# Four small re-arrangements around interleaved selective scans in an eight-image conv, attention and state-space kernel

## The chip, the cores and the metric

The kernel runs on one core of a Trainium2 chip, on a batch of eight images. The metric is the device time of one execution in microseconds (us), lower is better. A core has five instruction queues that the text names by their engine: PE (TensorE, matrix products, with its weight loads PEld), DVE (VectorE), ACT (ScalarE), POOL (GpSimd) and SP (SyncE, which here only issues DMAs). DMAs of convolution and projection weights are issued from ACT's queue, nearly all others from SP's.

## The reference

Each image has 256 channels and 32 x 32 = 1024 positions. Four residual layers follow one another; the first three see a group norm of their input.

```python
x = x + attention(gn(x))            # layer 0: 8 heads of 64, l2-normed q and k
x = x + conv3x3(gn(x), w1)          # layer 1
x = x + conv3x3(gn(x), w2)          # layer 2
x = x + mixer(gn(x))                # layer 3
# mixer(x): xs = x as 1024 tokens of 256 channels
xn = layernorm(xs)
xm = [mamba(xn[:, 64*i:64*i+64]) + skip * xn[...] for i in range(4)]   # 4 branches
Q  = gates from xm;  r = projections and depthwise convs of xm * sigmoid(Q), and of xs
xm2 = project(cat(xs, r)) + xs
x_out = cat(conv1d(xm2), mha(xm2)) @ fc_w.T + fc_b
out = project(layernorm(depthwise3x3(ln_hw(gelu(layernorm(x_out))))))
# mamba: u, z = xs @ inw;  u = silu(conv1d(u));  dt = softplus(...u...);  B, C = ...u...
#   h[t] = exp(dt[t]*A) * h[t-1] + dt[t]*u[t]*B[t];  y[t] = sum_s C[t]*h[t] + u*D   (16 states)
```

All arithmetic is in 32-bit floats.

## The kernel before

**Layers and stages.** For one image the front is `front_attention` and `front_convs` (layers 0 to 2). Then `scan_layers` norms the image and runs the four mamba branches. Then come `back_layers` (gates, projections, the mixer's attention), `back_out` (the `fcw` projection) and `back_end` (gelu, norms, the 3x3 depthwise convolution and the last projection). Front and back layers are "dense": PE carries most of them. A loop over images `b` puts the scans of image `b` beside the front of image `b + 1` and the back of image `b - 1`. For the last image (`b` = 7, counted from 0) there is no further front, so its scans stand beside the back of image 6 alone; the back of image 7 is written after all that.

**Handing out the scans.** `interleave(dense, scans, pace)` walks the dense stream, whose steps yield an estimated cost, and takes one step of the scan stream each time that the cost spent has grown by `pace`. `PACE` has one value per image: 1.8, then 2.78 six times, then 1.6. Within a queue, an instruction of a scan step is kept behind the dense instruction written ahead of it (`Paced`, `held`). Beyond that a scheduler decides the order on each engine when the program is built; on the chip every engine works through its list in order.

**Scans.** A scan works on 32 channels x 4 states in 128 partitions and 512 positions. A branch has 16 units: two halves `h` of the positions, four groups `q` of states, two pairs `gp` of channel groups. A unit takes: `load` and `load_dt` (DMAs of `du`, `bc` and `dt` from memory), `drive` (POOL, line 974: `hs = du * B`), `decays` (ACT: two times `da = exp(dt * A)` into PSUM), `scan` (DVE: two scans of 512), `weigh` (POOL, lines 1005 and 1006: keep the last state in `carry`, then `hs = hs * C`), and `add_up` (PE: `y += hs`). Tiles of `du` and `dt` are loaded once per half (at `q == 0`), one for each `gp`, and serve four units each; so units 0, 1 and 8, 9 of a branch load them, four DMAs for each tile. Each stage runs some units ahead:

```python
for ahead, stage in (
    (3, load), (1, load_dt), (0, decays), (0, None),
    (0, scan), (-1, weigh), (2, drive),
):
```

**A branch's front.** `branch_front` makes what the scans load, in six steps: project, convolve to `u`, `low` (B and C, stored as `bc`, line 865), `a` and an exponential, step sizes `dt` (stored as `dt_m`, line 818), and `dt * u` (stored as `du_m`, line 818). `fronts` gives the steps of the next branch due times in units of the running scans. `branch_back` multiplies by the gate `z` and projects once a branch has ended. Stores and loads of the scans, the small DMAs of the attentions (`sums`, `both`, `inv`, `rs`) and `mix` all stand in SP's one queue.

**The mix tensor.** `back_layers` ends with four 128 x 1024 tiles: two of the local convolution, two of the attention (`o3`). They are stored to memory as `mix` (line 1312), and `back_out` loads them again (line 1379) as input of the `fcw` projection. For images in the middle there is a whole front attention between the two.

**Buffers.** `wsp` (weight chunks), `hp` (`half_work`: the tiles `rs0` and `both`, which DMAs read), `dtp` (tiles `du` and `dt`, two each), `hsp` (six), `tp` (twelve 128 x 1026 tiles for nearly all dense work).

All of PE's, DVE's and ACT's instructions are issued through one wrapper and carry line 105 in the profile; there the tile names tell them apart.

Of the kernel before, what the change touches and what calls it, by code (L numbers as in the profile page):

```python
# [11 lines left out]
F32 = mybir.dt.float32  # L12
# [7 lines left out]
P = 128  # L20
C = 256
N = 1024
HALF = 512
# [10 lines left out]
def preact_stack(ctx: ExitStack, tc: tile.TileContext, I, out, cols):  # L34
# [7 lines left out]
    wp = ctx.enter_context(tc.tile_pool(name="wp", bufs=1))  # L42
    sp = ctx.enter_context(tc.tile_pool(name="sp", bufs=2))

    wsp = ctx.enter_context(tc.tile_pool(name="wsp", bufs=6))
    xp = ctx.enter_context(tc.tile_pool(name="xp", bufs=1))
    vp = ctx.enter_context(tc.tile_pool(name="vp", bufs=1))
    tp = ctx.enter_context(tc.tile_pool(name="tp", bufs=12))
    hp = ctx.enter_context(tc.tile_pool(name="hp", bufs=2))
    ps_big = ctx.enter_context(tc.tile_pool(name="ps_big", bufs=2, space=PSUM))  # L50
    ps_acc = ctx.enter_context(tc.tile_pool(name="ps_acc", bufs=1, space=PSUM))

# [11 lines left out]
    def work(name):  # L64
        return tp.tile([P, TP], F32, tag="t", name=name)
# [10 lines left out]
    def mwork(name):  # L76
        return mp.tile([P, N], F32, tag="m", name=name)
# [4 lines left out]
    def da_tile():  # L82
        return ps_da.tile([P, HALF], F32, tag="da", name="da")
# [730 lines left out]
    def store(br, name, src):  # L814

        br[name] = dp.tile([32, 2, 4, HALF], F32, tag=name, name=name + "_m")
        for h in range(2):
            nc.sync.dma_start(
                out=br[name][:, h].rearrange("d g n -> g d n"), in_=src[:, HALVES[h]]
            )  # L820

    def branch_front(i, xn, br):


        j, rows = i // 2, slice((i % 2) * 64, (i % 2) * 64 + 64)
        for h in range(2):
            ps = da_tile()
            tensor.matmul(
                ps,
                minw[rows, j, 0:P],  # L830
                inner(xn[j])[rows, HALVES[h]],
                start=True,
                stop=True,
            )
            scalar.copy(raw[:, 3 + h * HALF : 3 + (h + 1) * HALF], ps)
        yield
        u = mp.tile([P, N], F32, tag="u", name="u", bufs=2)
        uu = u[:, 0:N]
        scalar.activation(
            uu,  # L840
            raw[:, 3 : 3 + N],
            AF.Identity,
            bias=col("convb", i),
            scale=col("convw", 4 * i + 3),
        )
        for k in range(3):
            vector.scalar_tensor_tensor(
                uu, raw[:, k : k + N], col("convw", 4 * i + k), uu, ALU.mult, ALU.add
            )
        th = raw[:, 3 : 3 + N]  # L850
        scalar.activation(th, uu, AF.Tanh, scale=0.5)
        vector.scalar_tensor_tensor(uu, th, 1.0, uu, ALU.add, ALU.mult)
        br["u"] = u
        yield

        low = mwork("low")
        for h in range(2):
            ps = da_tile()
            tensor.matmul(
                ps[0 : 2 * DS], mxpw[:, i], u[:, HALVES[h]], start=True, stop=True  # L860
            )
            scalar.copy(low[0 : 2 * DS, HALVES[h]], ps[0 : 2 * DS])
        br["bc"] = dp.tile([DS, 2, 2, HALF], F32, tag="bc", name="bc")
        for k in range(2):
            nc.sync.dma_start(
                out=br["bc"][:, :, k],
                in_=low[k * DS : (k + 1) * DS].rearrange("s (h n) -> s h n", h=2),
            )
        yield

        a, dt = mwork("a"), mwork("dt")
        aa, ee, dd = a[:, 0:N], raw[:, 3 : 3 + N], dt[:, 0:N]
        for h in range(2):
            ps = da_tile()
            tensor.matmul(
                ps, mdtw[:, i], u[:, HALVES[h]], start=True, stop=True
            )
            vector.tensor_scalar_add(a[:, HALVES[h]], ps, col("dtb", i))  # L880
        scalar.activation(ee, aa, AF.Abs)
        scalar.activation(ee, ee, AF.Exp, scale=-1.0)
        yield
        vector.tensor_scalar_add(dd, ee, 1.0)
        vector.scalar_tensor_tensor(ee, dd, -1.0, ee, ALU.add, ALU.subtract)
        scalar.activation(dd, dd, AF.Ln)
        vector.tensor_sub(dd, dd, ee)
        vector.scalar_tensor_tensor(dd, aa, 0.0, dd, ALU.max, ALU.add)
        store(br, "dt", dd)
        yield  # L890
        vector.tensor_mul(aa, dd, uu)
        store(br, "du", aa)
        yield

    def branch_back(i, xn, br):
# [27 lines left out]
    def scan_steps(branches):  # L923
# [14 lines left out]
        def load_groups(u, name):  # L938
            br, g = branches[u["i"]], u["gp"] * 2
            if u["q"] == 0:  # L940
                t = dtp.tile([P, 2, HALF], F32, tag=name, name=name)
                src = br[name][:, u["h"], g : g + 2].rearrange("d g n -> d (g n)")
                for s in range(4):
                    nc.sync.dma_start(
                        out=t[s * 32 : s * 32 + 32].rearrange("d g n -> d (g n)"),
                        in_=src,
                    )
                br[name, u["gp"]] = t
            u[name] = br[name, u["gp"]]
# [80 lines left out]
        for n in range(-3, len(units) + 2):  # L1030
            done = None
            for ahead, stage in (
                (3, load), (1, load_dt), (0, decays), (0, None),
                (0, scan), (-1, weigh), (2, drive),
            ):
                if stage is None:
                    yield
                elif 0 <= n + ahead < len(units):
                    stage(units[n + ahead])
            if n % 2 and 0 <= n - 3 < len(units) - 1:  # L1040
                done = add_up(units[n - 3 : n - 1])
            yield done

    def scan_layers(img):


        xt = img.pop("x")
        img["stats"] = group_stats(img.pop("mv"), da_tile)
        xn = [xm_tile("xn0"), xm_tile("xn1")]
        for t in xn:  # L1050
            zero_ends(t)
        group_norm(tiles(xt), img["stats"], [inner(t) for t in xn])
        img["xd"] = xdp.tile([P, 2, N], F32, tag="xd", name="xd")
        nc.sync.dma_start(out=img["xd"], in_=xt)
        sq = [mwork("ln_sq"), mwork("ln_sq")]
        yield
        yield from layer_norm(
            [inner(t) for t in xn], sq, BY_HALF, da_tile, affine("norm_w", "norm_b")
        )
        yield  # L1060
        branches = [{} for _ in range(NB)]
        for _ in branch_front(0, xn, branches[0]):
            yield

        def fronts():
            for i in range(1, NB):
                for n, _ in enumerate(branch_front(i, xn, branches[i])):
                    yield 16 * i - 12 + 9 * n // 4

        front, ending, due, n = fronts(), iter(()), 0, 0  # L1070
        steps = scan_steps(branches)
        while True:
            next(ending, None)
            while due is not None and n >= due:
                due = next(front, None)
            if next(steps, END) is END:
                break
            yield
            done = next(steps)
            if done is not None:  # L1080
                ending = branch_back(done, xn, branches[done])
            n += 1
            yield
        yield from ending
        img["xm"] = xn
# [123 lines left out]
    def back_layers(img, exact=False):  # L1209
# [82 lines left out]
        yield from project("fpw", fd, evac_x2)  # L1292


        img["mix"] = xdp.tile([4, P, N], F32, tag="mix", name="mix")
        local = []

        def add_local():
# [9 lines left out]
                next(img["begin"])  # L1308
        while len(local) < 2:
            add_local()  # L1310
        for t, part in enumerate(local + img.pop("o3")):
            nc.sync.dma_start(out=img["mix"][t], in_=part[:, 0:N])

    def merge_weights():

# [58 lines left out]

    def back_out(img):

        srcs = [work("mix")[:, 0:N] for _ in range(4)]
        for t in range(4):
            nc.sync.dma_start(out=srcs[t], in_=img["mix"][t])
        yield 0  # L1380
        xo = img["xo"] = [work("xo")[:, 0:N] for _ in range(2)]

        def evac_fc(m, ps):
            scalar.activation(xo[m], ps, AF.Identity, bias=fc_b[:, m : m + 1])

        yield from project_both("fcw", srcs, evac_fc)
# [124 lines left out]
    PLACES = [1, 4, 4, 4, 4, 5, 6, 8, 9, 10, 11, 12, 13, 14, 15, 16]  # L1511
    PLACES += [18, 20, 22, 24, 26, 27, 28, 29]
    EARLY = 3
    PACE = [1.8] + [2.78] * (batch - 2) + [1.6]
    imgs = [{} for _ in range(batch)]
    drain(
        amid(front_attention(image_of(0), imgs[0]), merge_weights(), (8,)),
        front_convs(imgs[0]),
# [51 lines left out]
    again = nc.values_load(flag[0:1, 0:1], min_val=0, max_val=1)  # L1570
    with tc.If(again > 0):
        with tc.For_i(0, batch, 1) as i:
            img = {}
            src = x_in[bass.ds(i, 1)].rearrange("o (t p) n -> p (o t) n", p=P)
            dst = out[bass.ds(i, 1)].rearrange("o c n -> (o c) n")
            drain(front_attention(src, img, True), front_convs(img), scan_layers(img))
            drain(back_layers(img, True), back_out(img), back_end(img, dst))
# [109 lines left out]
```

## Time and profile before

| what | value |
|---|---|
| median of 3 runs | 6550.79 us (6543.21 to 6555.45) |
| the profiled execution's own time | 6534.17 us |
| its span in the trace | 6532.5 us |
| PE, DVE, ACT, POOL busy | 5503.0, 4003.1, 2701.2, 2737.3 us |
| clock granted to PE, mean | 0.91 of full speed |
| moved by DMA | 496 MB, 76 GB/s |

Busy time is summed per engine and averages over stages with different limits. The span begins with 375 us of the front of image 0 alone; seven stages with scans beside dense work follow, and one stage with dense work alone. A wait is put down to the engine whose event ended it. A record `x4` is four instructions of one kind merged; a 32-bit matmul shows as two.

### The profile page before, as it was taken

The page shows a single profiled execution, that of the slowest core. Times are in us where ns is not written, and L with a number is a line of the kernel's source. Part 1 is how long each engine was busy: PE and PEld are TensorE (multiplying, and loading weights), DVE is VectorE, ACT ScalarE, POOL GpSimd, SP SyncE. Part 2 cuts the span into 40 slices and gives each one's busy share as a digit, 9 for nine tenths or more (in the row PEclk, how much of TensorE's full clock was granted, in tenths as well). Part 3 has the DMA queues.
Part 4 walks back from the last instruction along what each step waited for, and adds up shares of the span by engine and source line. Part 5 has one row for each costly group of instructions (what it writes and reads, how often), then busy time and mean ns, then how long its engine had stood idle before and what let it go on. Part 6 is the DMA issues. An engine that isn't in the chain of part 4 may idle for free.

```text
span 6532.5 us, 52259 instructions
## 1 busy us (share of the span) xinstructions
PE 5503.0 (84%) x17318; PEld 1846.7 (28%) x17318; DVE 4003.1 (61%) x4613; ACT 2701.2 (41%) x3241; POOL 2737.3 (42%) x1302
## 2 busy tenths in 40 slices
PE   8886688899888988989889898899889898876496
PEld 2331133223332233222332233322332223311222
DVE  5247845577556775567756776567855777555622
ACT  3223424644255532644236442555326442344242
POOL 0006653634435353543517345263435435276500
PEclk9997889999899989999899998999899998988697
DMA  1022232323233132321223222231323212233301
GB/s 44 26 62 76 78 89 76 88 74 88 69 91 98 39 93 77 101 85 57 81 82 99 75 75 80 83 103 44 91 77 101 87 57 82 77 82 88 97 26 43
DMA packets 224761, 495.99 MB, mean 76 GB/s; under 512 B 61016, under 2 KB 102616, under 8 KB 223456
## 3 DMA queue, kind: packets, MB, share of 16 engines
q1 hardware_dynamic: 168032, 419.12, 22.2%
q10 hardware_dynamic: 56448, 73.43, 3.9%
q8 instruction: 139, 2.28, 0.1%
q14 instruction: 142, 1.16, 0.1%
HBM read 411.09 MB, written 72.88 MB: 74 GB/s over the span
## 4 chain that ended last, share of the span: by engine, by line
PE 53%; DVE 24%; issue 6%; DMA 6%; ACT 6%; POOL 4%; SPq 1%; ACTq 0%; DVEq 0%; POOLq 0%
PE big L105 33%; PE acc L105 11%; DVE hs L105 6%; PE da L105 5%; DVE p L105 4%; DVE dw L105 3%; POOL hs L1006 3%; PE y L105 3%; DVE u L105 2%; DVE t L105 1%; DMA du_m<-a 1%; POOL hs L974 1%; ACT p L105 1%; ACT da L105 1%; DMA dt<-dt_m 1%
## 5 line engine op out<-in xcount | busy, mean ns | idle before, releaser
L974 POOL TENSOR_TENSOR hs<-du,bc 128x1024 f32<-128x1024 f32 x512 | 1339.7, 2636 | 1623.2 <-DMA du<-du_m 683.0
L1006 POOL TENSOR_TENSOR hs<-hs,bc 128x1024 f32<-128x1024 f32 x512 | 1303.7, 2547 | 1027.7 <-DVE hs L105 841.2
L105 ACT ACTIVATE p<-big 128x1024 f32<-128x1024 f32 x1024 | 1038.5, 1021 | 735.0 <-PE big L105 724.2
L105 PE MATMUL acc<-p,v 128*64 128x512 f32 x4096 | 1151.8, 636 | 8.8 <-ACT both L105 6.0
L105 ACT ACTIVATE da<-dt,a_neg 128x512 f32<-128x512 f32 x1024 | 684.2, 686 | 1144.7 <-DVE hs L105 442.1
L105 PE MATMUL big<-im,w 128*128 128x512 f32 x2304 | 1104.0, 631 | 20.4 <-ACT im L105 20.4
L105 DVE TENSOR_TENSOR p<-p 128x1024 f32<-128x1024 f32 x448 | 720.0, 1607 | 295.2 <-ACT p L105 201.8
L105 DVE TENSOR_TENSOR_SCAN hs<-da,carry,hs 128x512 f32<-128x512 f32 x512 | 623.5, 1265 | 256.4 <-ACT da L105 176.0
L105 DVE TENSOR_TENSOR_SCAN hs<-da,hs 128x512 f32<-128x512 f32 x512 | 599.7, 1209 | 286.6 <-ACT da L105 267.6
L105 PE MATMUL big<-qk,qk 64*128 64x512 f32 x2048 | 647.9, 663 | 95.2 <-ACT p L105 85.5
L105 PE MATMUL y<-hs,sel 128*32 128x512 f32 x2048 | 454.0, 674 | 315.3 <-POOL hs L1006 314.8
L105 PE MATMUL big<-q,k 64*128 64x512 f32 x2048 | 616.8, 660 | 107.2 <-ACT p L105 60.6
L105 PEld LDWEIGHTS big<-im,w 128*128 128x128 f32 x2304 | 446.9, 201 | 689.5 <-issue 642.1
L1005 POOL COPY carry<-hs 128x2 f32<-128x2 f32 x256 | 104.2, 407 | 823.0 <-DVE hs L105 745.0
L105 PEld LDWEIGHTS acc<-p,v 128*64 128x64 f32 x4096 | 213.7, 137 | 820.3 <-issue 719.0
L105 PEld LDWEIGHTS big<-qk,qk 64*128 64x128 f32 x2048 | 178.2, 192 | 537.1 <-issue 280.1
L105 PEld LDWEIGHTS big<-q,k 64*128 64x128 f32 x2048 | 165.8, 190 | 535.5 <-issue 252.6
L105 DVE SCALAR_TENSOR_TENSOR dw<-xo,vec,dw 128x961 f32<-128x961 f32 (+1 forms) x128 | 247.8, 1972 | 16.4 <-ACT dw L105 15.2
L105 PEld LDWEIGHTS y<-hs,sel 128*32 128x32 f32 x2048 | 58.6, 112 | 616.7 <-POOL hs L1006 456.4
L105 PE MATMUL big<-xn,w 128*128 128x512 f32 x512 | 230.1, 601 | 0.0
L105 DVE SCALAR_TENSOR_TENSOR u<-raw,vec,u 128x1024 f32<-128x1024 f32 x96 | 136.2, 1419 | 87.1 <-ACT u L105 85.3
L105 PE MATMUL big<-w,xn 128*128 128x512 f32 x256 | 137.2, 687 | 42.6 <-ACT big L105 34.9
(214 smaller groups left out, 5085.5 us busy)
## 6 DMA issues: line engine op xcount, KB each, us to landing
bc<-bc SPq DMA_DIRECT2D x1024, 128.0 KB
du<-du_m SPq DMA_DIRECT2D x512, 128.0 KB
dt<-dt_m SPq DMA_DIRECT2D x512, 128.0 KB
w<-in_wc ACTq DMA_DIRECT2D x192, 192.0 KB
rs<-inv SPq DMA_DIRECT2D x64, 256.0 KB
dt_m<-dt SPq DMA_DIRECT2D x64, 256.0 KB
du_m<-a SPq DMA_DIRECT2D x64, 256.0 KB
mix<-mix SPq DMA_DIRECT2D x32, 512.0 KB
```

The source lines that it names most:

```text
L105: made = issue(*args, **kwargs)
L974: nc.gpsimd.tensor_mul(u["hs"], u["du"], both_groups(u["bc"][:, 0]))
L1005: nc.gpsimd.tensor_copy(carry[:, u["q"], g : g + 2], hs[:, :, HALF - 1])
L1006: nc.gpsimd.tensor_mul(hs, hs, both_groups(u["bc"][:, 1]))
```

## The change

- Weight chunks have five buffers for six, `half_work` tiles one for two. The tag `dt` gets three buffers for two; `du` keeps two.
- In `branch_front` the step that makes and stores `bc` is moved from third to last place.
- `load_dt` runs two units ahead for one.
- The due times of a branch's front, relative to its first unit, are listed as `FRONT`: -12, -10, -8, -7, -6, -2. Before they were -12, -10, -8, -6, -3, -1. A due time is that of the step after the one it is listed with.
- With `direct` set (images 6 and 7 of the eight), `back_layers` hands its four tiles to `back_out` on the chip, and `mix` is neither stored nor loaded.
- The last value of `PACE` is 1.1 for 1.6.

```diff
-    wsp = ctx.enter_context(tc.tile_pool(name="wsp", bufs=6))
+    wsp = ctx.enter_context(tc.tile_pool(name="wsp", bufs=5))
-    hp = ctx.enter_context(tc.tile_pool(name="hp", bufs=2))
+    hp = ctx.enter_context(tc.tile_pool(name="hp", bufs=1))
...
     def branch_front(i, xn, br):
...
         br["u"] = u
         yield
-        low = mwork("low")
...
-        yield
         a, dt = mwork("a"), mwork("dt")
...
         store(br, "du", aa)
         yield
+        low = mwork("low")
...
+        yield
...
-                t = dtp.tile([P, 2, HALF], F32, tag=name, name=name)
+                bufs = 3 if name == "dt" else 2
+                t = dtp.tile([P, 2, HALF], F32, tag=name, name=name, bufs=bufs)
...
-                (3, load), (1, load_dt), (0, decays), (0, None),
+                (3, load), (2, load_dt), (0, decays), (0, None),
...
-                for n, _ in enumerate(branch_front(i, xn, branches[i])):
-                    yield 16 * i - 12 + 9 * n // 4
+                for at, _ in zip(FRONT, branch_front(i, xn, branches[i])):
+                    yield 16 * i + at
...
-        img["mix"] = xdp.tile([4, P, N], F32, tag="mix", name="mix")
+        if not img.get("direct"):
+            img["mix"] = xdp.tile([4, P, N], F32, tag="mix", name="mix")
...
-        for t, part in enumerate(local + img.pop("o3")):
-            nc.sync.dma_start(out=img["mix"][t], in_=part[:, 0:N])
+        parts = [t[:, 0:N] for t in local + img.pop("o3")]
+        if img.get("direct"):
+            img["mix"] = parts
+            return
+        for t, part in enumerate(parts):
+            nc.sync.dma_start(out=img["mix"][t], in_=part)
...
     def back_out(img):
-        srcs = [work("mix")[:, 0:N] for _ in range(4)]
-        for t in range(4):
-            nc.sync.dma_start(out=srcs[t], in_=img["mix"][t])
+        srcs = img["mix"]
+        if not img.get("direct"):
+            srcs = [work("mix")[:, 0:N] for _ in range(4)]
+            for t in range(4):
+                nc.sync.dma_start(out=srcs[t], in_=img["mix"][t])
...
-    PACE = [1.8] + [2.78] * (batch - 2) + [1.6]
-    imgs = [{} for _ in range(batch)]
+    FRONT = (-12, -10, -8, -7, -6, -2)
+    PACE = [1.8] + [2.78] * (batch - 2) + [1.1]
+    imgs = [{"direct": b >= batch - 2} for b in range(batch)]
```

More of the change, by code (lines that the diff above doesn't have):

```diff
@@ L854, in branch_front @@
         yield
-        low = mwork("low")
[L857 to L868, printed above, removed]
-        yield
         a, dt = mwork("a"), mwork("dt")
@@ L892, in branch_front @@
         store(br, "du", aa)
+        yield
+        low = mwork("low")
+        for h in range(2):
+            ps = da_tile()
+            tensor.matmul(
+                ps[0 : 2 * DS], mxpw[:, i], u[:, HALVES[h]], start=True, stop=True
+            )
+            scalar.copy(low[0 : 2 * DS, HALVES[h]], ps[0 : 2 * DS])
+        br["bc"] = dp.tile([DS, 2, 2, HALF], F32, tag="bc", name="bc")
+        for k in range(2):
+            nc.sync.dma_start(
+                out=br["bc"][:, :, k],
+                in_=low[k * DS : (k + 1) * DS].rearrange("s (h n) -> s h n", h=2),
+            )
         yield
@@ L1572, in preact_stack @@
         with tc.For_i(0, batch, 1) as i:
-            img = {}
+            img = {"direct": True}
             src = x_in[bass.ds(i, 1)].rearrange("o (t p) n -> p (o t) n", p=P)
```

## The prediction, made before the changed kernel was run

> **What bounds the kernel now.** I read the page's header and slices first, then the busy table by stretches, then the waits, then the queue and engine timelines around single waits. The storing of each image's scan input (`xd<-xt`, line 1054, at 375, 1029, 1805, 2570, 3340, 4101, 4862 and 5624 us) cuts the span into stages.
>
> ```profile
> span 6532.5 us, 52259 instructions
> ...
> PE   8886688899888988989889898899889898876496
> ...
> POOL 0006653634435353543517345263435435276500
> ```
>
> PE is nearly full up to the 37th slice, then falls to 6, 4, 9, 6. The busy table says how much (columns: stretch, length, then busy us with counts for PE, PEld, DVE, ACT, POOL, then granted clock, DMA share, GB/s):
>
> ```profile
> 4101.20:4862.40 761.20, 670.46 (x2160) 225.63 (x2160) 505.64 (x573) 337.07 (x406) 343.93 (x160) 0.94 0.28 81
> ...
> 5623.70:6207.50 583.80, 376.15 (x1156) 119.17 (x1158) 334.85 (x346) 231.02 (x285) 320.19 (x159) 0.78 0.31 87
> 6207.50:6532.50 325.00, 246.58 (x812) 90.95 (x812) 82.30 (x127) 107.29 (x106) 4.53 (x2) 0.85 0.10 33
> ```
>
> A middle stage is bound by PE (670 of 761 us, so some 90 us idle). The last scanned image is not: PE has 376 of 584 us and POOL, the scans' busiest engine, 320. That stretch is a chain of scans through ACT, DVE, POOL, PE and the queue of SP, with the back layers of image 6 (counted from 0) woven in. After it the back layers of image 7 run alone, 325 us. The waits:
>
> ```profile
> PE y L105 <- POOL hs L1006: 314.8, 114, 19.7
> ...
> ACT da L105 <- DMA dt<-dt_m: 276.0, 26, 26.6
> ```
>
> ACT, which also makes the attention's `p` for PE, stands 276 us behind step sizes. Why, SP's timeline shows at one of them, with ACT's line below it:
>
> ```profile
> 5752.03 1.17 SPq L818 DMA_DIRECT2D dt_m<-dt  x2
> 5753.25 2.60 SPq L959 DMA_DIRECT2D bc<-bc  x4
> 5755.96 7.52 SPq L944 DMA_DIRECT2D dt<-dt_m  x8
> ```
> ```profile
> 5764.52 1.30 ACT L105 ACTIVATE da<-dt,a_neg 128x512 f32<-128x512 f32 x2 [16.45 <-DMA dt<-dt_m]
> ```
>
> The loads that unit 8 of a branch needs (its second half) stand in SP's queue behind the store of the next branch's step sizes, which waits for DVE. The same happens at 5882 and 6005 us.
>
> **The Trainium skill.** "DMA: Bandwidth & Descriptors", section "Anatomy of one DMA", says that a DMA's semaphore wait is spent on the issuing sequencer before dispatch; the fence above agrees, since the loads are issued only after the waiting store. "TensorE: Matmul & The Clock Gate", Part 1, says that an idle window of about 3.4 us halves the clock; the trace agrees (four `y` records take 1.05 us in a busy stretch, 1.92 after 10 us of idleness), so idle PE costs a little more than itself. "GPSIMD Engine Reference", section 4.1, calls POOL about twice as slow as DVE on two inputs; here 2.36 us against 1.22 for 128x1024. "Perfetto Trace Analysis", section "Optimization Strategy", says that regular bubbles can mean too few buffers; that fits the two `dt` tiles, both in use until the half's last two units.
>
> **The change, part by part.**
>
> *Order of a branch's front, due times, third `dt` tile, loads two units ahead.* No instruction is added. In the written order of instructions DVE now finishes a branch's step sizes before it takes the `y` of the half (line 1029), where it took that `y` in between at branches 2 and 3 of the last image; so the drain scans, `y`, step sizes, store, load, `da` is cut. The `du` store moves with it. On SP both stores, and after them the `bc` store, now stand ahead of the last `du` loads and of the `dt` loads of the second half, so a late DVE would hold POOL instead. They stand there two units before use (about 10 us of POOL work), against the some 10 us that store and load take (5752.0 to 5764.5, with the loads between). I take most of each drain off: POOL's idle time there, 14.6 and 12.1 us, plus some lag of ACT.
>
> In the middle stages PE hardly feels this. In the stage 4101 to 4862 I can tie to `dt` only the 6.05 us at 4375 (ACT late with `big`) and perhaps half of the 9.6 us at 4200; the largest wait, 10.05 us at 4689, comes from DVE busy with `dw`. Taken: 5 us for each of six stages, 30 us; bounds -2 and +15 each. In the first stage with scans (375 to 1029, 167 us of PE idleness, 80 us of ACT waiting for `dt`): 10 us, bounds -5 and +40.
>
> *Five weight tiles for six, one `half_work` for two.* A convolution uses a chunk every 5.2 us, so four loads ahead are still 21 us; the waits show PE held by no weight load. A `both` or `rs` copy comes every eight attention steps (16.5 us apart at least), and its DMAs take about 4. Cost 0; the cover is gone if SP stands longer than that, and then ACT and PE wait. Bounds -10 and +40 us in all, within the low end below.
>
> *Inputs of the last projection kept on the chip (images 6 and 7).* 16 DMAs of 512 KB go, no instruction comes. For image 7:
>
> ```profile
> 6414.10 2.79 PE L105 MATMUL acc<-p,v 128*64 128x512 f32 x12
> 6430.01 15.58 PE L105 MATMUL big<-mix,w 128*128 128x512 f32 x32 [13.11 <-issue]
> ```
>
> Three quarters of these matmuls need only `local` and the first `o`, ready at 6417. The last quarter needs the `o` that DVE finishes at 6429.5, and 3 us of PE after that: done at 6432.5 instead of 6445.6, a gain of **13 us**. For image 6 it is in the sum below.
>
> *Pace 1.6 to 1.1.* This is the large item, with both signs. At 1.6 the scans (148 steps, 237 of cost) outlast the 226 that the back layers of image 6 add up to. At 1.1 they ask for 163 and are handed out inside the attention. The order of PE's instructions in the changed program bears it out: the last `y` stand among the `fcw` matmuls, and then all of `back_end` of image 6 comes before the first matmul of image 7's back layers. So the end is a sum in series. With E the end of the last scan on DVE (6209 us before):
>
> - last scan to the last `xn` of the branch, 6209.0 to 6223.3: 14.3
> - `few_inv` to `o`, now behind it on DVE, 6422.1 to 6429.5: 7.4
> - the last `fcw` matmuls: 3
> - `back_end`, alone on PE, 6445.6 to 6523.4 as image 7 shows: 77.8
> - back layers of image 7, first `qdw` matmul to the end, 6221.8 to 6532.5: 310.7, less 13.1
>
> Together 400.1. It pays if E falls below 6132. Before, from 5716.5 us, the halves of eight units took 49, 49, 82, 46, 76, 62, 86 and 42 us; POOL needs 39 (2 x 2.36 and a copy). The halves of 76 and 82 hold a drain and about twelve attention steps; those of 62 and 86 were held by `back_out` and by `back_end`'s `dw` on DVE. In the new order the second half's `y` have no attention between, the third and fifth keep their branch front (about 15 us of DVE and ACT in a row), and the last has fourteen attention steps of 2.1 us. I take 47, 42, 55, 43, 55, 43, 47, 53: E = 6101.5, end 6501.6, a gain of **31 us**. Bounds for E: 6065 (every half near POOL's 43) and 6150 (fronts and drains as before).
>
> Sum: 31 + 30 + 10 = 71 us off the profiled 6532.5, so 6461; its own time is 6534.17. The median of the runs, 6550.79, lies 16.6 above that; against it: **6480 us**.
>
> **The rivals.**
> (a) *Only the end counts*: a PE-bound stage gives ACT's waits back elsewhere, middle 0. For it: PE's named waits are mostly not on `dt`. Gain 31: 6520.
> (b) *The middle gains in earnest*: the 20 us waits for `dt` also delay the `y` on PE (28 to 29 us a stage). At 15 us for six stages, 25 in the first and 31: 146, so 6405. Against it: those `y` mostly follow DVE's `dw`.
> (c) *Slower*: the scans do not keep the denser pace, because DVE's and ACT's order, not the number handed out, sets it. The 78 us in which `back_end` of image 6 now stands alone on PE are then not repaid. Decides from E = 6132; with the old halves to unit 48 (6081), then 47 and 40, E is 6168 and the end 36 us later: 6587. For it: POOL idled 10 us at 5806 and 12 at 5844 with no late DMA. Against it: at 1.6 it was the attention between the scans that held them.
> (d) *Not what it says*: the third tile may be idle because SP's queue, not the tile, holds the load. Then the drains stay (some 27 us), E is about 6128, nothing comes in the middle: 6546.
>
> **How the numbers follow.** Forecast 0.45, (a) 0.2, (b) 0.15, (c) 0.12, (d) 0.08. The range runs from (b), 6405, to 6555, which takes in (d) and the mild part of (c). A measurement of this kernel tells about 0.2% (13 us) from no change. Faster by more: the forecast, (a), (b) and little of (d), 0.83; within: 0.06; slower: 0.11, nearly all of (c).
>
> **What would show it.** Right: the waits of `da` on `dt` fall from 276 us to well under 150; no `mix` DMA in the last two images; the last scan ends near 6100, less what the earlier stages gained; then about 80 us with PE at a third or less; the stages stay near 755. Wrong: `du` waits on POOL inside an image where `dt` waits were; ACT waiting for `sums` or weights; a scan stretch still longer than 416 us; or back layers of the two images overlapping after all.

## The result and the profile after

| | before | after |
|---|---|---|
| median of four runs | 6547.0 us | 6601.33 us |
| range | 6533.63 to 6555.45 | 6598.77 to 6612.32 |
| span of the profiled execution | 6532.5 us | 6600.8 us |
| clock granted to PE | 0.910 | 0.906 |

The ratio is 1.0083 (95%: 1.0065 to 1.01): the change made the kernel 0.8% slower, where the prediction had 1% faster. The experiments below split this: the third tile with earlier loads, the smaller pools and the kept inputs alone make the kernel 1.5% faster; the due times and the pace take that and more.

The page's header and slices of the kernel after:

```profile
span 6600.8 us, 52312 instructions
...
PE   8886688998889979899789988899798897856686
...
POOL 0007653634345252644526344352535435277400
```

The hole near the end is still there: where PE's digits were 7, 6, 4, 9 they are 5, 6, 6, 8. Cut by the store of the scan input, the stages took these times (the last column is a kernel of the experiments):

| stage (image of the scans) | before | after | front_pace_undone |
|---|---|---|---|
| 0 | 653.6 | 660.4 | 644.3 |
| 1 | 776.5 | 762.3 | 745.8 |
| 2 to 6, mean | 763.7 | 776.3 | 760.4 |
| 7 | 908.8 | 923.3 | 881.7 |

Of the 68 us that the span grew, 63 arose in stages 2 to 6, 14.5 in the last and 7 in stage 0; stage 1 gave 14 back. The busy table of the kernel after (columns as before: stretch, length, busy us with counts for PE, PEld, DVE, ACT and POOL, clock, DMA share, GB/s) shows a middle stage and the two halves of the last one:

```profile
4119.50:4899.30 779.80, 676.35 (x2160) 228.41 (x2160) 500.04 (x573) 337.72 (x406) 341.63 (x160) 0.93 0.28 79
5677.50:6195.30 517.80, 353.68 (x1022) 93.64 (x1022) 287.05 (x273) 212.39 (x269) 318.82 (x159) 0.78 0.31 82
6195.30:6600.80 405.50, 289.22 (x944) 120.11 (x944) 120.70 (x200) 125.66 (x123) 3.75 (x2) 0.81 0.09 26
```

The middle stage has the same instructions as before (2160 matmuls, 160 on POOL). Of its 18.6 us, 12.7 are PE's idleness (103.4 for 90.7); in the other 5.9 PE does the same matmuls at a clock of 0.93 for 0.94. In the last stage the last scan began 517.8 us after the start of the stage, and ended 66.2 us sooner than before; but 405.5 us followed its beginning, and what followed its end was 80.7 us longer than before.

The waits of ACT, a part of the list (total, times, longest):

```profile
ACT da L105 <- PE big L105: 293.8, 32, 21.1
...
ACT da L105 <- DMA bc<-bc: 170.4, 11, 17.0
...
ACT da L105 <- DMA dt<-dt_m: 142.5, 23, 27.2
...
ACT low L105 <- PE da L105: 104.7, 28, 10.0
```

The sign that the prediction had asked for seems to be there: `da` waits for `dt` 142.5 us for 276.0. But the list names only one releaser for each wait, and in the kernel before it hides another:

```profile
4703.05 13.48 ACTq L159 DMA_DIRECT2D w<-in_wc  x3
4716.74 1.30 ACT L105 ACTIVATE da<-dt,a_neg 128x512 f32<-128x512 f32 x2 [20.11 <-DMA dt<-dt_m]
```

ACT goes on 0.2 us after weight loads that it issued itself (`ACTq` is the queue on which ACT issues the chunks of weights). Eight of the 26 waits put down to `dt` before, 167.0 of the 276.0 us, end in this way, all in middle stages and stage 0, with 16 to 27 us each. After, two of those put down to `dt` do (49.1 us), and all eleven put down to `bc` (170.4; before it was 47.5 of 67.9). Waits that end with ACT's own loads are thus 214.5 us before and 219.5 after, and what is left of the waits for `dt` is 109.0 before and 93.4 after. So the sign came about mostly because waits of one kind got another name. The rest of the list doesn't tell why the kernel is slower either: front_pace_undone of the experiments, which is faster than both, has 142.3 us behind `dt` and 261.3 for PE, where the kernel after has 142.5 and 293.8 and the kernel before 276.0 and 173.9. A wait that is gone from the list is no gain until the stage is shorter.

What became of the drain in the last image, SP's timeline shows (start, duration, queue, line, operation, number of DMAs), and ACT's below it:

```profile
6020.56 0.36 SPq L945 DMA_DIRECT2D dt<-dt_m  x1
6042.85 1.23 SPq L818 DMA_DIRECT2D dt_m<-dt  x2
6046.39 1.11 SPq L818 DMA_DIRECT2D du_m<-a  x2
6047.55 1.79 SPq L945 DMA_DIRECT2D dt<-dt_m  x3
6050.56 1.27 SPq L889 DMA_DIRECT2D bc<-low  x2
```
```profile
6047.38 0.57 ACT L105 COPY low<-da 32x512 f32<-32x512 f32 x1 [6.80 <-PE da L105]
...
6058.41 1.30 ACT L105 ACTIVATE da<-dt,a_neg 128x512 f32<-128x512 f32 x2 [7.16 <-DMA bc<-low]
```

One `dt` tile takes four DMAs. The first is issued at 6020.9; then SP stands for 21.9 us at the store of the next branch's step sizes, stands again for their product (`du_m`, DVE was done with it at 6046.4), and issues the other three at 6047.6. The third tile is there, two units ahead as asked, and its load is cut apart by two stores. The same happens at 5883 us, where the rest follows 22.6 us after the first.

### The profile page after: what moved, and what is told of

The parts are those of the page before. It is cut to its first block, busy times and chain, and to the rows that moved or that the text cites. A ratio compares the mean times of both kernels' runs of the same rounds, so it can differ in the third digit from the quotient of the medians.

```text
span 6600.8 us, 52312 instructions
## 1 busy us (share of the span) xinstructions
PE 5518.5 (84%) x17318; PEld 1854.8 (28%) x17318; DVE 3970.4 (60%) x4613; ACT 2703.0 (41%) x3241; POOL 2726.9 (41%) x1302
## 3 DMA queue, kind: packets, MB, share of 16 engines
q1 hardware_dynamic: 165728, 410.73, 21.9%
## 4 chain that ended last, share of the span: by engine, by line
PE 51%; DVE 23%; ACT 7%; issue 6%; DMA 6%; POOL 5%; SPq 1%; ACTq 0%; DVEq 0%; POOLq 0%
PE big L105 33%; PE acc L105 10%; DVE hs L105 6%; PE da L105 5%; DVE p L105 4%; PE y L105 3%; POOL hs L1007 3%; POOL hs L975 2%; DVE dw L105 2%; DVE u L105 2%; DVE t L105 2%; DMA du_m<-a 1%; ACT p L105 1%; ACT da L105 1%; DMA du<-du_m 1%
## 5 line engine op out<-in xcount | busy, mean ns | idle before, releaser
L975 POOL TENSOR_TENSOR hs<-du,bc 128x1024 f32<-128x1024 f32 x512 | 1311.9, 2581 | 1697.7 <-DMA bc<-bc 716.7
L105 PE MATMUL big<-im,w 128*128 128x512 f32 x2304 | 1131.3, 644 | 75.2 <-ACT im L105 71.2
L105 DVE TENSOR_TENSOR p<-p 128x1024 f32<-128x1024 f32 x448 | 693.0, 1547 | 306.2 <-ACT p L105 222.8
L1006 POOL COPY carry<-hs 128x2 f32<-128x2 f32 x256 | 126.6, 495 | 794.9 <-DVE hs L105 741.9
L105 DVE SCALAR_TENSOR_TENSOR dw<-xo,vec,dw 128x992 f32<-128x992 f32 (+1 forms) x128 | 245.6, 1960 | 27.4 <-ACT dw L105 26.3
L105 PE MATMUL da<-xn,w_minw 64*128 64x512 f32 x256 | 166.1, 763 | 56.6 <-DVE hs L105 55.6
```

The costliest lines, as they stand in the source:

```text
L105: made = issue(*args, **kwargs)
L975: nc.gpsimd.tensor_mul(u["hs"], u["du"], both_groups(u["bc"][:, 0]))
L1006: nc.gpsimd.tensor_copy(carry[:, u["q"], g : g + 2], hs[:, :, HALF - 1])
```

## The experiments

Medians are given; the kernel before, run again beside each group of experiments, took 6541 to 6546 us. "Stages" are those of the table above. Where a kernel changes only due times, its list `FRONT` is the edit.

### Which part costs: undone one at a time, and one alone

**pace_undone.** The kernel after, with

```diff
-    PACE = [1.8] + [2.78] * (batch - 2) + [1.1]
+    PACE = [1.8] + [2.78] * (batch - 2) + [1.6]
```

> The changed kernel with the last image's pace back at 1.6, all else as changed. Theory 1 (the dense pace loses: the back layers of image 6 left alone cost 78 us, and the scans came in only 66 us): the last stage falls from 923 us to about 896 (908.8 of the kernel before less the 13 us of the transfers left out), the six middle stages stay 8 us longer each, the whole run takes about 6574 us. Rival 2 (the dense pace gains as it was meant to, and the loss in the last stage comes from the new order of the front or from the buffers): the last stage grows to 940 or more, the run to over 6615 us.

6564.9 us; last stage 885.9 for 923.3. Theory 1 holds: the dense pace costs 36 us. The last scan comes 54.3 us later (572.1 after the stage's start for 517.8), and what follows it is 91.7 us shorter (313.8 for 405.5).

**dt_bufs_undone.** The kernel after, with

```diff
-    wsp bufs=5, hp bufs=1, dt bufs=3, (2, load_dt)
+    wsp bufs=6, hp bufs=2, dt bufs=2, (1, load_dt)
```

> The changed kernel with two dt tiles, loads one unit ahead, six weight tiles and two half_work tiles again; order of the front, due times, pace and kept inputs as changed. Theory A (the front's new order and its due times make the middle stages longer): the stages stay near 775 us, the run within 15 us of 6601. Theory B (fewer weight and half_work tiles, or loads issued earlier, make them longer): the stages fall to 761 to 765 us, the run to about 6545 us.

6576.7 us: 25 less than after, stages 2 to 6 near 770. Neither theory is met: inside the new front the tile, its earlier loads and the pools lose together, but most of the loss stays without them.

**front_undone.** The kernel after, with `bc` made ahead of the step sizes again and the old due times:

```diff
-                for at, _ in zip(FRONT, branch_front(i, xn, branches[i])):
-                    yield 16 * i + at
+                for n, _ in enumerate(branch_front(i, xn, branches[i])):
+                    yield 16 * i - 12 + 9 * n // 4
```

> The changed kernel with the front of a branch in its old order (bc made and stored ahead of the step sizes) and at its old due times; third dt tile, smaller pools, pace and kept inputs as changed. Theory A (the front's order and due times cost the middle stages 8 to 19 us each): the stages fall to about 761 us, the run to about 6545 us. Theory B (buffers or earlier loads): the stages stay near 775 us, the run near 6600 us.

6482.3 us, 119 less than after, and more than Theory A asked for. The front is the loss; without it the rest of the change gains.

**direct_alone.** The kernel before, with `mix` of images 6 and 7 kept on the chip.

> The kernel before with only the inputs of the last projection of images 6 and 7 kept on the chip. Theory (as predicted: 16 transfers fewer, image 7's last projection no longer waits for them): 13 us less, about 6534 us. Rival (the four kept tiles stay taken from the pool of twelve until the projection has read them, and other work waits for a free one): 0, or up to 10 us slower.

6526.2 us, ratio 0.997 (0.9958 to 0.9981): 20 us. The last stage took 886.5 for 908.8. The prediction had put 13 on image 7 and left image 6's share in the sum of the last stage.

**pools_alone.** The kernel before, with `wsp` 5 for 6 and `hp` 1 for 2.

> The kernel before with five weight tiles for six and one half_work tile for two, nothing else. As predicted: no cost, within 10 us of 6546. Rival (ACT or PE waits for weights or for row sums): up to 40 us slower.

6547.4 beside 6541.1, ratio 1.0009 (0.9997 to 1.0021): what was measured can't be told from a cost of 0.

**pace_alone.** The kernel before, with pace 1.1 for the last image.

> The kernel before with only the last image's pace at 1.1. Theory (back layers of image 6 alone for 78 us, scans sooner by less than that): last stage about 909 + 37 = 946 us, less if the scans were the end before; the run 6575 to 6585 us. Rival (the pace pays by itself, and it was the third tile and the kept inputs that took its gain): 6530 us or less.

6580.4 beside 6543.4: 37 us lost here too, last stage 933.4. The pace costs the same with and without the other parts.

### Order or due times

All kernels from here on have the pace at 1.6 unless said.

**front_pace_undone.** What is left of the change with neither the new front nor the dense pace: third `dt` tile, loads two ahead, smaller pools, kept inputs.

> The kernel before with the third dt tile, loads two units ahead, the smaller pools and the kept inputs, and neither the new front nor the dense pace. Theory (each part costs or saves what undoing it alone showed: the dense pace costs some 36 us, the new front 119): 6482 - 36 = about 6446 us, last stage about 885 us. Rival (the dense pace pays where the front does not stand in its way): 6482 us or more, last stage 917 us or more.

6440.6 us, ratio 0.9845 (0.9829 to 0.9861), as the theory had it.

**old_order_new_times** and **new_order_old_times** put one half of the front back each.

> As front_pace_undone (pace 1.6, old order of the front, with bc ahead of the step sizes), but the parts of the front at the new due times -12, -10, -8, -7, -6, -2. Theory T (the due times cost it: five parts within six units of a branch crowd DVE and ACT): about 6565 us, as the changed kernel with the pace undone. Theory O (the order of the parts costs it: bc last, and the step sizes' sums right behind the convolution): about 6446 us, middle stages 755 to 762 us.

> As front_pace_undone (pace 1.6), but the front in its new order (step sizes first, bc last) at the old due times -12, -10, -8, -6, -3, -1. Theory T (due times): about 6446 us. Theory O (order): about 6565 us; with bc stored at -3 it can be worse, since its load is issued at the same unit: up to 6620 us.

| | old times | new times |
|---|---|---|
| old order | 6440.6 | 6567.7 |
| new order | 6484.3 | 6564.9 (pace_undone) |

The due times cost 127 us in the old order and 81 in the new. The order costs 44 at the old times and nothing (-3) at the new ones. Theory T holds for nearly all of it. What the order costs by itself this table can't say: a list goes by place, so at the old times the new order also stores the step sizes at -8 for -6 and `du` at -6 for -3. That puts both stores ahead of loads in SP's queue, and the place of `du` alone is the largest piece below.

### Which due time

**store_early** moves the step sizes' store alone: `(-12, -10, -8, -7, -3, -1)`.

> As front_pace_undone (old order of the front, pace 1.6), but one due time moved: the part that ends in the store of the step sizes at -7 for -6, so times -12, -10, -8, -7, -3, -1. In SP's queue that store then stands ahead of the du and both dt loads for the second half of the branch in hand; at -6 it stood behind the du loads and the first dt load. Theory Q (the queue: a store that waits for DVE holds these loads, and with them ACT and PE): most of the 127 us of the new due times, 6520 to 6570 us. Rival C (crowding: the due times cost because du, or the next branch's first part, come sooner): within 20 us of 6440.

6456.7 us, +16: an eighth of the loss, where theory Q had most of it. The edit moved less than was expected. In the middle stages one store of three moves, ahead of two DMAs of a tile's load, and the other two keep their place among the `dt` loads. In the last image the store does stand ahead of six to eight of the eight `dt` loads of a half, and that stage isn't longer (878.4 us for 881.7). The cost is in the first two stages (657.3 and 755.9 for 644.3 and 745.8).

**du_early** moves the part with `dt * u` and its store: `(-12, -10, -8, -6, -6, -1)`.

> As front_pace_undone, with the du part at -6 for -3, right behind the store of the step sizes: times -12, -10, -8, -6, -6, -1. Theory F (the new times cost because the next branch's first matmuls come at -2): within 15 us of 6441. Rival D (du's store behind its own DVE product now stands ahead of the second dt load of the half, and DVE does both parts in a row): 6480 to 6540 us.

6520.4 us, +80: Rival D, the largest piece. (The profiled execution, 6504.2, is the lowest of the 13 runs.)

**first_early** and **first_earlier** move the first part of the next branch: `(-12, -10, -8, -6, -3, -2)` and `(..., -3, -3)`.

> As front_pace_undone, with the first part of the next branch (two matmuls from xn into da tiles, two copies to raw on ACT) at -2 for -1: times -12, -10, -8, -6, -3, -2. Theory F: PE's wait with these matmuls for the scans on DVE goes from 14 to about 50 us (weight loads beside it from 24 to about 80), middle stages 768 to 775 us, the run 6500 to 6550. Rival D: within 15 us of 6441.

> As first_early, with that part at -3 (together with du's part). Theory F, by parity: at -1 and -3 the matmuls stand behind the y matmuls that end the step before, PE has waited there for a later product on POOL already, so both da tiles are free or nearly; at -2 they stand in front of them. Then -3 costs no more than -1: within 15 us of 6441, the wait at about 15 us. Rival (earlier is worse, whatever the step): 6550 us or more.

6465.3 and 6425.7 us: +25 at -2, and 15 less than at -1 when it comes at -3. PE's wait for the scans at `da` grew in both, to 71.6 and 76.2 us from 39.0, so that wait does not separate them and my reading of it falls. What the odd unit does to the order on the engines stays open.

Alone, the three times cost 16, 80 and 25, together 121; measured together in the old order they cost 127. There they add up.

**du_store_apart.** As du_early, with the store alone put back to -3 (the list gets one entry more, `(-12, -10, -8, -6, -6, -3, -1)`):

```diff
         vector.tensor_mul(aa, dd, uu)
+        yield
         store(br, "du", aa)
```

> As du_early, with the product dt * u on DVE still at -6, but its store issued at -3 as in front_pace_undone (a yield between the two; the first branch of an image takes no extra step). The order on DVE is that of du_early, but for a few swaps in the last image, and the order on SP that of front_pace_undone. Theory Q (in SP's queue du's store waits for DVE in front of the second dt load of the half): back to within 15 us of 6441, ACT's waits for dt from 233 to about 145 us. Rival V (the product in front of two scans on DVE is the cost): stays within 20 us of 6520, with few waits for dt.

6441.0 us: all 80 us are back, and the waits of `da` for `dt` are 120.3 us for 233.4. In stages 2 to 6 DVE, PE and POOL work in the same order in both kernels, and SP's list differs in the three stores of `du` alone; on ACT up to three weight loads of a stage have a slightly different place. With that reserve it is the place of two DMAs, once a branch, in SP's queue: these five stages are 46.5 us longer in du_early, and PE falls back 43.3 of them in the 40 us around each of those stores. The same spot of a middle stage in du_early, SP and then ACT:

```profile
3839.07 0.77 SPq L945 DMA_DIRECT2D dt<-dt_m  x2
3848.39 1.19 SPq L818 DMA_DIRECT2D dt_m<-dt  x2
3851.68 1.12 SPq L818 DMA_DIRECT2D du_m<-a  x2
3852.85 2.54 SPq L945 DMA_DIRECT2D dt<-dt_m  x2
```
```profile
3849.61 9.05 ACTq L159 DMA_DIRECT2D w<-in_wc  x2
3864.77 1.30 ACT L105 ACTIVATE da<-dt,a_neg 128x512 f32<-128x512 f32 x2 [14.55 <-DMA dt<-dt_m]
```

and in du_store_apart:

```profile
3786.01 0.77 SPq L946 DMA_DIRECT2D dt<-dt_m  x2
3795.24 1.19 SPq L818 DMA_DIRECT2D dt_m<-dt  x2
3796.47 1.47 SPq L946 DMA_DIRECT2D dt<-dt_m  x2
3798.04 5.61 SPq L961 DMA_DIRECT2D bc<-bc  x4
3805.05 1.06 SPq L818 DMA_DIRECT2D du_m<-a  x2
```
```profile
3796.46 9.04 ACTq L159 DMA_DIRECT2D w<-in_wc  x2
3806.13 0.69 ACT L105 ACTIVATE da<-dt,a_neg 128x512 f32<-128x512 f32 x1 [9.05 <-PE y L105]
```

Counted from the tile's first two DMAs, the step sizes' store comes 9.2 to 9.3 us later in both. The second two come 13.8 us later in du_early and 10.5 in the other, and the `da` that need them 25.7 and 20.1. The store of `du` has no reader for three units yet; it waits 2 us for DVE, and with it the load that ACT needs next. Four of the six middle stages of du_early have such a wait, of 13.9 to 14.6 us; du_store_apart has none. There ACT is late with that `da` too, but for a weight load of its own. The Trainium skill, "DMA: Bandwidth & Descriptors", section "Anatomy of one DMA", says that the semaphore wait of a DMA is spent on the issuing sequencer before dispatch. This trace agrees: between 3849.6 and 3851.7 us SP issues nothing, until DVE has ended the product.

**store_late** `(-12, -10, -8, -5, -3, -1)` and **new_order_late**, the new order with `(-12, -10, -5, -4, -3, -2)`, put the stores behind the loads of the half.

> As store_early with the same part at -5 for -6: times -12, -10, -8, -5, -3, -1. The store then stands behind both dt loads of the second half, and five units ahead of its own first load. Theory Q: the remaining waits for dt at mid-branch go as well, 6405 to 6430 us. Rival C: within 10 us of 6440. If step sizes come too late for the next branch: over 6450 us.

> The changed kernel at pace 1.6 with its own new order of the front, but stores behind the second half's loads: times -12, -10, -5, -4, -3, -2 for -12, -10, -8, -7, -6, -2. Theory Q (not the order but the place of the stores in SP's queue): 125 to 155 us less than the 6565 us at the new times, so 6410 to 6440 us. Rival O (the new order costs by itself, 44 us as at the old due times): 6480 us or more.

6490.5 and 6518.7 us. Theory Q misses in both; the numbers lie where the other readings had them, step sizes that come too late (over 6450) and rival O (6480 or more). In store_late the long waits for `dt` in the last image are gone, all but one of 6.9 us, and the last stage is 876.4 for 881.7; but stages 3 to 6 are 768 to 775. What made these longer stays open. So a place behind all loads is not the rule either: the queue's order explains the largest piece of the old order's loss, and not every due time. The new order takes 46 us less at late times than at its own (6564.9), and still 78 more than the old order at the old times; its first part at -2 is in that, which alone cost 25.

In the kernels with the new order, all but dt_bufs_undone, most middle stages have an ACT wait of 15.3 us that front_pace_undone, store_early and first_early don't have there. In the kernel after:

```profile
4821.64 5.49 ACTq L159 DMA_DIRECT2D w<-in_wc  x2
4827.33 1.30 ACT L105 ACTIVATE da<-dt,a_neg 128x512 f32<-128x512 f32 x2 [15.31 <-DMA bc<-bc]
```

The wait is put down to `bc`, which `da` doesn't read. ACT goes on 0.2 us after its own two weight loads are issued, and each of these was issued 0.04 us after a matmul `big<-im,w` had ended on PE (4821.60 and 4826.76). So I read it as a weight load that waited for a free tile with ACT behind it. That is argued from the trace, not tested. Nor does this wait explain the loss: new_order_old_times has it too, with stages 2 to 6 at 762.2 us, and dt_bufs_undone, with six weight tiles, has one of about 25 us in each of these stages instead.

### The pace

**pace_1_4** is front_pace_undone at 1.4; **pace_1_8** is first_earlier at 1.8.

> As front_pace_undone with the last image's pace at 1.4. Theory (a pace costs nothing as long as the scans asked for, 148 steps of 1.4 = 207, fill nearly all of the 226 that the back layers add up to; what is left alone, 19, is won back by scans that end some 23 us sooner): within 8 us of 6440. Rival (the loss grows evenly from 1.6 to 1.1, some 40 us): 6455 us.

> As first_earlier, with the last image's pace at 1.8 for 1.6. Theory (best where the scans asked for, 148 steps times the pace, just fill the 226 of the back layers, which is at 1.53): 266 of 226, so the back layers are all out well before the scans end, and the last scans run with nothing beside them: 5 to 25 us more than 6426. Rival (1.4 and 1.1 cost time in a straight line, and the line goes on): 6406 us.

6460.3 us, +20, and 6412.9 us, -13 against first_earlier. Both theories miss, and the rivals, a straight line (6455 and 6406), come near: the cost falls from 1.1 (+36 to +42) over 1.4 to 1.8, about evenly, and no best value shows at 1.6. pace_1_8 is the fastest kernel here, ratio 0.9802 (0.9777 to 0.9827).

## Why the prediction was wrong

**The account.** From the kernel left over (6440.6): three due times 16 + 80 + 25, measured together +127; new order at these times -3; dense pace +36: 6601, the kernel after. From the kernel before to 6440.6 it is -103: kept inputs -20, pools +6 (not told from 0), so the third tile with loads two ahead made some -89. That is a remainder, for the tile was not run alone. Nor does it show in the waits that the tile was for: without those that end with ACT's own weight loads, `da` waits 112.1 us for `dt` in front_pace_undone and 109.0 before, while those behind `dt` and `bc` that do end so fell from 214.5 to 104.2 us. Why they fell stays open. Between the profiled executions of direct_alone and front_pace_undone there are only 54 us, most of them in stages 0, 1 and 3 (-9, -22, -10), as the former was the lowest of its runs and the latter the highest.

**Order, due times, tile and loads (predicted -40, and most of the 31).** This is the step that failed. It bundled four edits as one gain. The tile and the loads were worth about twice the 40; the due times ate it all. The prediction saw that both stores would stand ahead of the loads, and set against it that they "stand there two units before use (about 10 us of POOL work), against the some 10 us that store and load take". That margin was mis-sized: its ten us begin at 5752.0, when the store is issued, and leave out the time for which SP stands in front of it until DVE is done. The rest of a tile's load stands behind it for that time too: 3.3 us more in the pair above, and in the last image of the changed kernel 26.6 us between the first DMA of a tile's load and the rest. And in the middle stages, where "PE hardly feels this", stages 2 to 6 became 13 us longer, not 5 shorter. For them the mechanism is shown in the old order alone, where du_early's waits for `dt` are 233.4 us, for 120.3 with the store put back. In the new order it isn't: there the waits for `dt` in stages 2 to 6, without those that end with ACT's own weight loads, are 43 us at the old times (new_order_old_times) and at the new ones (pace_undone), while these stages took 762.2 and 777.6 us. By what way the due times cost 81 us there stays open. The start of the reading was weak as well: of the 276 us "behind step sizes" 167.0 end with weight loads of ACT. Rival (d) named the place, SP's queue that holds the loads; it gave it a lost gain, where it was a loss.

**The last stage (predicted -31, measured +14.5).** The sum in series was right: it gave E + 400.1, and 404.2 us came after E, the end of the last scan; PE waits twice for `dw` there, 29.0 us each, once in each lone `back_end`. Image 7's last matmuls end 16.8 us after the attention, not 28.7:

```profile
6495.92 2.79 PE L105 MATMUL acc<-p,v 128*64 128x512 f32 x12
6498.65 7.13 PE L105 MATMUL big<-local,w 128*128 128x512 f32 x16
6505.62 3.60 PE L105 MATMUL big<-o,w 128*128 128x512 f32 x8
6511.80 3.70 PE L105 MATMUL big<-o,w 128*128 128x512 f32 x8 [2.58 <-DMA x_in<-xd]
```

That is 11.9 for the 13 predicted. The term that failed is E. The halves of eight units were to take 47, 42, 55, 43, 55, 43, 47, 53 us, 385 together; from the first scan of one to that of the next they took 51, 38, 73, 69, 67, 41, 51, 45, which is 435. They began 8.5 us earlier in the stage, so E came 519.0 us after the stage's start for 477.8. The threshold, 6132, is 508 on that scale: 11 us too late and 4 more in the tail make up about the 14.5. The third and fifth halves hold the drain that was to be cut and was not (the timeline of SP shown first is from the fifth). Rival (c) had this mechanism, a `back_end` alone on PE that isn't repaid, and 36 us; the runs gave 36, 37 and 42. That the figures agree is in part luck: (c) came to its 36 with E at 6168, where the run has 6143 on that scale, and with the kept inputs in the sum.

**What held.** The pools at 0 (measured +6, with an interval that takes in no change), and the kept inputs, which were worth more than the 13 us said for image 7. The prediction's signs of being wrong showed in part: a scan stretch of 435 us, over the 416, and ACT behind weight loads; and the stages did not stay near 755.

## What to carry to other kernels

In a queue that serves stores and loads, order by who reads next: a store with no reader soon that waits for an engine holds every load behind it, and can cut the load of one tile in two. Cost each edit of a bundle by itself, and look at each queue's order around the late instruction rather than at how many units lie between. When a stretch of scans is compressed, ask what will run alone afterwards: here each microsecond that the dense pace won on the scans cost 1.7 behind them (54.3 and 91.7). And when a wait of an engine that issues DMAs is put down to a transfer, look whether its own issue ended last.

## What the runs showed that was not expected

- The same two DMAs of a branch, in nearly the same program but for their place on one queue, are worth 80 us of 6441 (du_early, du_store_apart).
- The due times add up nearly exactly in the old order (121 in parts, 127 together), and the pace costs about the same in three settings (36, 37, 42), while tile and front don't add: the third tile with earlier loads gains some 89 us, a remainder, with the old front and loses 25, with its pools, in the new one.
- ACT's own weight loads hold ACT for 9 to 16 us at a time in middle stages, in the kernel before too (13.5 us at 4703, in a wait that the list puts down to `dt`). The prediction asked whether PE waits for weights, and listed ACT waiting for them as a sign of being wrong; it did not see that ACT already did.
